# A third transpose by way of DRAM strips in the first layer's pipeline, and a new place for the router's products

## The chip, the core and the metric

The kernel runs on one core of a Trainium2 chip. The metric is the device time of one execution in microseconds (us); it is the median of repeated runs. The engines are named as in the profile: PE is TensorE's matmuls, PEld its weight loads, DVE is VectorE, ACT ScalarE, POOL GpSimd, SP SyncE, which here does nothing but issue DMA transfers. All data are float32.

## What is computed

Two layers follow each other on x of shape 4 x 1024 x 256. Each adds an attention and a feed-forward branch to x:

```python
xn = layernorm(x)
# layer 0: causal attention and a dense FFN on the same xn
q, k, v = xn @ Wq, xn @ Wk, xn @ Wv
att = softmax(where(causal, q @ k.T / sqrt(256), -inf))
x = x + layernorm(att @ v + v, gamma, beta) @ Wfc + bfc + relu(xn @ W1 + b1) @ W2 + b2

xn = layernorm(x)
# layer 1: gated attention (GAU) on layernorm(xn), and 8 experts, the best 2 per row
x = x + gau(layernorm(xn, ln1_w, ln1_b)) + experts(xn)
# experts: scores = softmax(xn @ Wg.T); of the best 2, weights scaled to sum 1
#   h1, h3 = (xn @ W1 + xn @ A1 @ B1 + b1), (xn @ W3 + xn @ A3 @ B3 + b3)
#   y = (silu(h1) * h3) @ W2 + (...) @ A2 @ B2 + b2
```

## The kernel before, in words

**Tiling.** A sequence has 1024 rows, eight tiles of 128 rows, taken in pairs. A pair tile u (0 to 15) is pair p = u % 4 of sequence b = u // 4, 256 rows. The first stage (layer 0, lines 244 to 796) is a loop over u; the second stage (from line 806) does layer 1.

**An iteration u of the first stage**, in the order of the text (lines 732 to 792) and in the order in which TensorE runs it:

- `turns` (L546): the softmax results att of u, made in the iteration before, are transposed on TensorE into PSUM (pt) and copied to attT. For p > 0 and u > 1 (`far(u)`) only the last two tiles go this way. The older part was written to DRAM (`atd`) by `bands` (L515) and read back in strips, `band`, so laid out that VectorE's transpose (which turns 32x32 blocks) leaves a full transpose. `weighted` (L556) does that transpose (L566) and multiplies attT by xn into pz: first the products with the tiles turned on TensorE (L571), then those with the band (L574).
- `hidden` (L532) in two halves: the first layer of the FFN, products pm (L539), relu on ScalarE into hT. The first half stands among the transposes at the iteration's start, the second half ahead of `finish`.
- `queries(u + 1)` (L472), then `scores(u + 1)` (L482): products sc, mask, maximum, exp, normalisation into att, of the next pair tile.
- `norms_turn(u - 1)` (L631): the result of `norms` of the pair tile before, xl, is transposed on TensorE by four instructions (L636) into PSUM and copied by ScalarE (L641), for sequence 0 into `xl0`, which stays, otherwise into `xlT`, which is also stored in DRAM (`xld`, L643) for the second stage. `logits(u - 1)` (L647) multiplies it by the router's and the qk weights (pl, L653).
- `first(u + 3)` (L439): layer norm of a later pair tile, xn. For u > 2 its xn is written to DRAM (`keep`, L429) and read back in four strips of 128-byte rows (`strip`, L436); `first_turn` (L452) turns the strips on VectorE (L455).
- `finish(u)` (L582): for each of the two tiles 8 products po with w2 (L590) and 2 products pv (L594), then the sums.
- `merge` (L393) folds an expert's low-rank factors into its weights: it loads wt and lt from DRAM early; `multiply` makes the small products pab and pc (L411 to L414), VectorE adds them to wt (L417), and two stores follow.
- `norms(u)` (L607): layer 1's two norms of the new x into xl (VectorE, L621) and xr.
- Once a sequence is through, `route` and `send` (L661, L691) pick experts and slots, and `rows_out` scatters the rows by indirect DMA on POOL's queue.

**What sets the order.** Each engine runs its instructions in the order in which they were issued. That order is not the text's own: a planner in the framework goes through all traced instructions with a model of their costs, and gives each engine next, of the instructions which it holds to be ready, the one that stands earliest in the text. `tc.issue_after(ins)` queues the instructions of its block behind `ins` on the same engine. SP is one such engine: if a DMA waits for its source, those behind it on SP wait too. A tile taken from a pool with `bufs=n` under a tag waits until one of the n slots is free.

**Slots.** att takes four slots of 4 KB per partition under the tag "att"; the bands that come back from DRAM, and `early` (rows of biases at the start), take theirs from the same four. strip has one slot, xl one, PSUM tiles named by `bank` share four banks, sc and merge's products two double banks.

Of the kernel before, what the change touches and what calls it, by code (L numbers as in the profile page):

```python
# [9 lines left out]
F32 = mybir.dt.float32  # L10
# [7 lines left out]
P = 128  # L18
B, N, D = 4, 1024, 256
NT = N // P  # L20
DC = D // P
# [4 lines left out]
E, HID, R = 8, 512, 16  # L26
# [41 lines left out]
def block_kernel(ctx: ExitStack, tc: tile.TileContext, x, wq, wk, wv, wfc, w1, w2, wqk, wvl, wg,  # L68
                 wo, wr, ew, el, eb2, cols, rows, rope, posb, out):
    nc = tc.nc  # L70
    pers = ctx.enter_context(tc.tile_pool(name="pers", bufs=1))
    small = ctx.enter_context(tc.tile_pool(name="small", bufs=3))
    NP = NT // 2
# [101 lines left out]
    yg = dram.tile([NF * TB + NHB * HB, D], F32, name="yg")  # L175
    xnd = dram.tile([B * NP, 2 * P, D], F32, name="xnd")
    atd = dram.tile([B * NP, 2 * P, (NP - 1) * 2 * P], F32, name="atd")
    xld = [dram.tile([P, DC, N], F32, name=f"xld{b}") for b in range(B)]
# [59 lines left out]
    with ExitStack() as l0:  # L238
# [7 lines left out]
        def bank(shape, name):  # L246
            return p_mm.tile(shape, F32, tag="mm", name=name)
# [17 lines left out]

        early = act.tile([P, 3 * D], F32, tag="att", name="early", bufs=4)
        nc.scalar.dma_start(out=wq_s, in_=wq)
# [125 lines left out]
        def merge(u, after):  # L393
            e, c = u // DC, u % DC
# [12 lines left out]
            def multiply():  # L407

                pab, pc = (p_sc.tile([P, 2, HID], F32, tag="sc", name=n) for n in ("pab", "pc"))
                pa, pb, pc = pab[:, 0], pab[:, 1], pc[:, 0].rearrange("p (i d) -> p i d", i=2)  # L410
                nc.tensor.matmul(pa, f1[:, ts(c, P)], f1[:, D : D + HID], start=True, stop=True)  # L411
                nc.tensor.matmul(pb, f3[:, ts(c, P)], f3[:, D : D + HID], start=True, stop=True)
                for i in range(2):
                    nc.tensor.matmul(pc[:, i, :], f2[:, ts(2 * c + i, P)], f2[:, HID : HID + D],  # L414
                                     start=True, stop=True)
                for k, p in enumerate((pa, pb, pc.rearrange("p i d -> p (i d)"))):
                    nc.vector.tensor_tensor(wt[:, k, :], p, wt[:, k, :], ALU.add)  # L417
                nc.sync.dma_start(
                    out=wm13[e, :, 0:EB1].rearrange("p (k c w) -> p k c w", k=2, c=DC)[:, :, c, :], in_=wt[:, 0:2, :])
                nc.sync.dma_start(out=wm2[e, :, ts(c, HID)], in_=wt[:, 2, :])  # L420
# [6 lines left out]

        def keep(u):
            nc.sync.dma_start(out=xnd[u].rearrange("(i p) d -> p i d", p=P), in_=xns[u])  # L429

        def strip(u):
            keep(u)
            w = strips[u] = act.tile([P, DC, 2 * P], F32, tag="strip", name="strip", bufs=1)
            src = xnd[u].rearrange("(i r) (c j a) -> j r c i a", r=32, c=DC, a=32)
            for j in range(4):
                nc.sync.dma_start(out=w[32 * j : 32 * j + 32].rearrange("r c (i a) -> r c i a", a=32), in_=src[j])  # L436


        def first(u):  # L439
# [9 lines left out]
            if u > 2:  # L449
                strip(u)  # L450

# [30 lines left out]
        def scores(u, qT):  # L482
            b, p = divmod(u, NP)
            atts = []
            for i in range(2):
# [10 lines left out]
                nc.vector.tensor_reduce(nmax, sc[:, :n], AX.X, ALU.max, negate=True)  # L496
                att = act.tile([P, N], F32, tag="att", name="att", bufs=4)
                rsum = small.tile([P, 1], F32, tag="rsum", name="rsum")
# [16 lines left out]
        def bands(u, i, att):  # L515
# [4 lines left out]
            if i == 0:  # L520
# [4 lines left out]
                bands.xn2, bands.got = xn2, []  # L525
            got = act.tile([P, N], F32, tag="att", name="band", bufs=4)[:, 0:w]
            src = there.rearrange("(i r) (j k) -> j r i k", r=32, j=4)
# [54 lines left out]
        def finish(u, hT, zT):  # L582
# [3 lines left out]
            for i in range(2):  # L586
# [6 lines left out]
                for c in range(DC):  # L593
                    nc.tensor.matmul(pv, zT[:, c, ts(i, P)], vo_s[:, c, :, :],  # L594
                                     start=(c == 0), stop=(c == DC - 1))
                nc.vector.tensor_tensor(xt, po[:, i, :], xt, ALU.add)
# [10 lines left out]
        def norms(u):  # L607
# [20 lines left out]
            nc.gpsimd.tensor_tensor(both, both, row("ln2_b").unsqueeze(1).to_broadcast([P, 2, D]), ALU.add)  # L628
            return xl

        def norms_turn(u, xl):  # L631
            b, p = divmod(u, NP)
            pt = bank([P, DC, 2 * P], "pt")
            for i in range(2):
                for c in range(DC):
                    nc.tensor.transpose(pt[:, c, ts(i, P)], xl[:, i, ts(c, P)], ident)  # L636
            if b == 0:
                xlT = xl0[:, :, ts(p, 2 * P)]
            else:
                xlT = act.tile([P, DC, 2 * P], F32, tag="xlT", name="xlT", bufs=1)  # L640
            nc.scalar.copy(xlT, pt)  # L641
            if b:
                nc.sync.dma_start(out=xld[b][:, :, ts(p, 2 * P)], in_=xlT)  # L643
            return xlT
# [87 lines left out]
        for u in range(U):  # L732
# [7 lines left out]
            if u == 1:  # L740
                for k in range(3):
                    keep(k)
                fold_second(raw)
# [15 lines left out]
            if u + 1 < U:  # L759
                qT = queries(u + 1)  # L760
            if u:
                xlT = norms_turn(u - 1, xl)
            zT = weighted(u, attT)
            if u:
                logits(u - 1, xlT, lgs)
            ready = scores(u + 1, qT) if u + 1 < U else None
            hidden(u, hT, range(IC // 4, IC // 2))
            if u + 3 < U:
                first(u + 3)
            if p == 1 and b:  # L770
                send(b - 1, *routed)
# [610 lines left out]
```

## Time and profile before

| | us |
|---|---|
| median of 3 timed runs | 1124.15 |
| lowest and highest | 1123.61, 1127.02 |
| the profiled execution, whole | 1128.42 |
| its span, first to last instruction | 1126.7 |

The granted TensorE clock was 0.998 of full speed on the mean. The first stage's last pv instruction begins at 503.0 us; layer 1's products start at 503.4 us.

TensorE's timeline gives the length of an iteration, from the start of merge's products (L411) to their next start:

| iteration | p | from, us | length, us | att read back through DRAM |
|---|---|---|---|---|
| 4 | 0 | 143.76 | 26.33 | no |
| 5 | 1 | 170.09 | 30.10 | 256 columns |
| 6 | 2 | 200.19 | 33.12 | 512 columns |
| 7 | 3 | 233.31 | 29.87 | 768 columns |

In the lines of a timeline the first number is the start in us from the span's start, the second the length of the group, then engine, line, operation and tiles (output<-inputs), the shapes, and how many of them follow each other. A bracket at the end is the idle time before it and what ended it. `SPq` is SP issuing a DMA; the transfer itself goes on afterwards. A product of float32 stands in the trace as two matmul instructions, a transpose as one; the counts are of instructions. Lines of a windows view give: the window, its length, the busy time of PE, PEld, DVE, ACT and POOL with the number of instructions, the granted clock, the mean busy share of the 16 DMA engines, and GB/s.

### The profile page before, as it was taken

Reading aid. Unit: us, or ns where it says so; the run is one execution under the profiler, and the core shown is the slowest. Engines: PE = TensorE matmul, PEld = TensorE weight load, DVE = VectorE, ACT = ScalarE, POOL = GpSimd, SP = SyncE. Lnnn points to the kernel's source line nnn. Section 1 sums busy time; section 2 is a strip of 40 time slices with the busy share of each in tenths; the row PEclk is TensorE's granted clock in tenths of the full one; section 3 lists DMA queues with packets and bytes.
Section 4 is the critical chain, followed back from the end, with each engine's and each line's share of the span. In section 5 each row is a group of like instructions: output and inputs, shape, how many; then the busy total and the mean of one; then the engine's idle time right before and its main releaser. Section 6 shows DMA issues by size and latency. Waiting matters only on the chain. (4 is left out here: it accounts for less than half of the span.)

```text
span 1126.7 us, 15401 instructions
## 1 busy us (share of the span) xinstructions
PE 1106.9 (98%) x5132; PEld 867.4 (77%) x5132; DVE 555.4 (49%) x1533; ACT 288.7 (26%) x758; POOL 177.7 (16%) x216
## 2 busy tenths in 40 slices
PE   8999999999999999999999999999999999999997
PEld 6788888888888888774688888888888884655645
DVE  5444554455444454547575623322332326677946
ACT  3323333333323333225211111111111113121121
POOL 2200002222032114141000000000000004453410
PEclk9999999999999999999999999999999999999999
DMA  8735434553455334420648786777777621322301
GB/s 308 200 100 160 129 99 149 159 178 119 132 162 155 94 128 141 158 96 33 222 101 290 212 269 190 241 227 221 238 228 223 231 85 57 121 76 75 95 28 37
DMA packets 186801, 173.77 MB, mean 154 GB/s; under 512 B 113888, under 2 KB 156384, under 8 KB 181600
## 3 DMA queue, kind: packets, MB, share of 16 engines
q1 hardware_dynamic: 99216, 137.89, 37.9%
q10 hardware_dynamic: 81360, 18.10, 7.5%
q0 software_dynamic: 6144, 16.79, 4.5%
q8 instruction: 41, 0.67, 0.3%
q14 instruction: 40, 0.33, 0.1%
HBM read 122.78 MB, written 51.02 MB: 154 GB/s over the span
## 5 line engine op out<-in xcount | busy, mean ns | idle before, releaser
L957 PE MATMUL p<-xT,w 128*128 128x256 f32 (+1 forms) x1152 | 241.2, 368 | 0.0
L957 PEld LDWEIGHTS p<-xT,w 128*128 128x128 f32 x1152 | 209.4, 190 | 26.9 <-issue 0.3
L1036 POOL DMA_INDIRECT y<-yg,slot x64 | 65.3, 1021 | 491.0 <-DVE v L1116 421.2
L962 ACT ACTIVATE s<-p,w 128x256 f32<-128x256 f32 (+1 forms) x144 | 58.8, 459 | 314.3 <-PE p L957 228.4
L965 DVE SCALAR_TENSOR_TENSOR g<-p,w,s 128x256 f32<-128x256 f32 (+1 forms) x144 | 60.8, 463 | 159.1 <-PE p L957 156.8
L978 PE MATMUL py<-w,g 128*128 128x256 f32 x544 | 123.4, 379 | 0.0
L539 PE MATMUL pm<-xnT,w_s 128*128 128x256 f32 x512 | 118.5, 379 | 0.0
L590 PE MATMUL po<-w_s,hT 128*128 128x256 f32 x512 | 116.1, 380 | 0.0
L978 PEld LDWEIGHTS py<-w,g 128*128 128x128 f32 x544 | 102.9, 190 | 14.2 <-DVE g L965 0.3
L590 PEld LDWEIGHTS po<-w_s,hT 128*128 128x128 f32 x512 | 96.9, 190 | 20.1 <-issue 8.0
L539 PEld LDWEIGHTS pm<-xnT,w_s 128*128 128x128 f32 x512 | 95.6, 192 | 11.6
L714 POOL DMA_INDIRECT xg<-xr,put x64 | 63.9, 998 | 209.0 <-ACT hT L542 138.2
L492 PE MATMUL sc<-xnT,qT 128*128 128x256 f32 (+1 forms) x320 | 65.8, 361 | 0.0
L542 ACT ACTIVATE hT<-pm,colt 128x256 f32<-128x256 f32 x128 | 53.9, 466 | 42.2 <-PE pm L539 42.2
L1114 PE MATMUL pv<-wvl_s,xl 128*128 128x512 f32 x128 | 58.1, 599 | 3.4 <-DVE v L1116 3.1
L594 PE MATMUL pv<-vo_s,zT 128*128 128x512 f32 x128 | 60.1, 592 | 0.0
L1232 PE MATMUL pj<-wo_s,gd 128*128 128x256 f32 x256 | 57.0, 381 | 2.6 <-DVE o L1234 2.1
L492 PEld LDWEIGHTS sc<-xnT,qT 128*128 128x128 f32 x320 | 54.6, 191 | 6.0 <-ACT qT L479 0.2
L1185 PE MATMUL pg<-xl,wg_s 128*128 128x512 f32 x128 | 57.5, 593 | 0.0
L1232 PEld LDWEIGHTS pj<-wo_s,gd 128*128 128x128 f32 x256 | 48.0, 190 | 10.2 <-DVE o L1234 3.3
L980 DVE TENSOR_TENSOR yt<-py,w 128x512 f32<-128x512 f32 (+1 forms) x36 | 23.8, 662 | 59.0 <-PE py L978 59.0
L603 DVE SCALAR_TENSOR_TENSOR x<-pv,rs,x 128x256 f32<-128x256 f32 x32 | 15.5, 484 | 72.1 <-ACT rs L189 47.7
(256 smaller groups left out, 1351.8 us busy)
## 6 DMA issues: line engine op xcount, KB each, us to landing
w<-wm SPq DMA_DIRECT2D x36, 1028.0 KB
w<-wm SPq DMA_DIRECT2D x36, 640.0 KB
wt<-in_ew_dram SPq DMA_DIRECT2D x16, 768.0 KB
wm<-wt SPq DMA_DIRECT2D x16, 512.0 KB
xt<-xg ACTq DMA_DIRECT2D x128, 64.0 KB
yg<-yt ACTq DMA_DIRECT2D x32, 256.0 KB
xnd<-xn SPq DMA_DIRECT2D x16, 256.0 KB
wm<-wt SPq DMA_DIRECT2D x16, 256.0 KB
```

What stands on the lines that cost most here:

```text
L492: nc.tensor.matmul(sc[:, kp * 2 * P : kp * 2 * P + w], qT[:, c, ts(i, P)], xnTs[b * NP + kp][:, c, 0:w], start=(c == 0), stop=(c == DC - 1))
L539: nc.tensor.matmul(pm[:, j, :], w1_s[:, c, ts(2 * m2 + j, P)], xnTs[u][:, c, :], start=(c == 0), stop=(c == DC - 1))
L590: nc.tensor.matmul(po[:, i, :], hT[:, m, ts(i, P)], w2_s[:, m, :], start=(m == 0), stop=(m == IC - 1))
L594: nc.tensor.matmul(pv, zT[:, c, ts(i, P)], vo_s[:, c, :, :], start=(c == 0), stop=(c == DC - 1))
L714: w = nc.gpsimd.indirect_dma_start(out=xg, out_offset=bass.IndirectOffsetOnAxis(ap=put[:, b * NT + t : b * NT + t + 1], axis=0), in_=xrs[b ...
L957: nc.tensor.matmul(p[:, j, :], w13[:, w0 : w0 + P], xT[:, c, :], start=(c == 0), stop=(c == DC - 1))
L962: nc.scalar.activation(s[:, j, :], p1[:, j, :], AF.Silu, bias=w13[:, EB1 + m : EB1 + m + 1])
L965: up.g = nc.vector.scalar_tensor_tensor(g[:, m, :], p3[:, j, :], w13[:, EB3 + m : EB3 + m + 1], s[:, j, :], ALU.add, ALU.mult).ins
L978: down.last = nc.tensor.matmul(py[:, k, :], g[:, m, ts(k, P)], w2[:, m * D : (m + 1) * D], start=(m == 0), stop=(m == EC - 1)).ins
L1036: w = nc.gpsimd.indirect_dma_start(out=ys[b][:, t, k, :], out_offset=None, in_=yg, in_offset=bass.IndirectOffsetOnAxis(ap=slot[:, n : n + ...
L1114: nc.tensor.matmul(pv, a.xl[:, c, ts(t, P)], wvl_s[:, c, :], start=(c == 0), stop=(c == DC - 1))
L1232: nc.tensor.matmul(pj, a.gd[:, m, ts(n, P)], wo_s[:, m, :], start=(m == 0), stop=(m == HC - 1))
```

## The change

It touches the first stage alone.

- xl of sequences 0 to 2 (pair tiles 0 to 11) is written to a new DRAM tensor `xlr` at the end of `norms`, read back in strips as xn is, and turned on VectorE straight into xl0 or xlT. The four TensorE transposes, their PSUM bank and ScalarE's copy stay for sequence 3 alone. `keep` and `strip` now take the place and the rows as arguments; `strip` returns its tile.
- For these pair tiles `norms_turn` and `logits` stand behind the second half of `hidden` and `first(u + 3)` in the text, ahead of `send` and of `finish` with its po products, instead of around `weighted`. In iterations 13 to 15 they stay where they were.
- `merge`'s products are queued behind the last pv product of `finish` (`finish.last`), in all iterations but the last.
- att gets two slots of its own, the bands that come back two smaller ones (768 columns, tag "band", shared with `early`), strip two slots instead of one.

```diff
--- before.py
+++ after.py
@@ -174,6 +174,7 @@
     xg = dram.tile([E * RS, D], F32, name="xg")
     yg = dram.tile([NF * TB + NHB * HB, D], F32, name="yg")
     xnd = dram.tile([B * NP, 2 * P, D], F32, name="xnd")
+    xlr = dram.tile([B * NP, 2 * P, D], F32, name="xlr")
     atd = dram.tile([B * NP, 2 * P, (NP - 1) * 2 * P], F32, name="atd")
     xld = [dram.tile([P, DC, N], F32, name=f"xld{b}") for b in range(B)]
 
@@ -263,7 +264,7 @@
             for _ in range(n):
                 keep_busy.last = nc.tensor.matmul(pw, idle[:, 0:P], idle, start=True, stop=True).ins
 
-        early = act.tile([P, 3 * D], F32, tag="att", name="early", bufs=4)
+        early = act.tile([P, 3 * D], F32, tag="band", name="early", bufs=2)
         nc.scalar.dma_start(out=wq_s, in_=wq)
         load_x(0, 0)
         nc.sync.dma_start(out=wk_s, in_=wk)
@@ -408,11 +409,12 @@
 
                 pab, pc = (p_sc.tile([P, 2, HID], F32, tag="sc", name=n) for n in ("pab", "pc"))
                 pa, pb, pc = pab[:, 0], pab[:, 1], pc[:, 0].rearrange("p (i d) -> p i d", i=2)
-                nc.tensor.matmul(pa, f1[:, ts(c, P)], f1[:, D : D + HID], start=True, stop=True)
-                nc.tensor.matmul(pb, f3[:, ts(c, P)], f3[:, D : D + HID], start=True, stop=True)
-                for i in range(2):
-                    nc.tensor.matmul(pc[:, i, :], f2[:, ts(2 * c + i, P)], f2[:, HID : HID + D],
-                                     start=True, stop=True)
+                with tc.issue_after(finish.last) if u + 1 < U else nullcontext():
+                    nc.tensor.matmul(pa, f1[:, ts(c, P)], f1[:, D : D + HID], start=True, stop=True)
+                    nc.tensor.matmul(pb, f3[:, ts(c, P)], f3[:, D : D + HID], start=True, stop=True)
+                    for i in range(2):
+                        nc.tensor.matmul(pc[:, i, :], f2[:, ts(2 * c + i, P)], f2[:, HID : HID + D],
+                                         start=True, stop=True)
                 for k, p in enumerate((pa, pb, pc.rearrange("p i d -> p (i d)"))):
                     nc.vector.tensor_tensor(wt[:, k, :], p, wt[:, k, :], ALU.add)
                 nc.sync.dma_start(
@@ -425,15 +427,16 @@
 
 
 
-        def keep(u):
-            nc.sync.dma_start(out=xnd[u].rearrange("(i p) d -> p i d", p=P), in_=xns[u])
-
-        def strip(u):
-            keep(u)
-            w = strips[u] = act.tile([P, DC, 2 * P], F32, tag="strip", name="strip", bufs=1)
-            src = xnd[u].rearrange("(i r) (c j a) -> j r c i a", r=32, c=DC, a=32)
+        def keep(there, rows):
+            nc.sync.dma_start(out=there.rearrange("(i p) d -> p i d", p=P), in_=rows)
+
+        def strip(there, rows):
+            keep(there, rows)
+            w = act.tile([P, DC, 2 * P], F32, tag="strip", name="strip", bufs=2)
+            src = there.rearrange("(i r) (c j a) -> j r c i a", r=32, c=DC, a=32)
             for j in range(4):
                 nc.sync.dma_start(out=w[32 * j : 32 * j + 32].rearrange("r c (i a) -> r c i a", a=32), in_=src[j])
+            return w
 
 
         def first(u):
@@ -447,7 +450,7 @@
             for i in range(2):
                 normalise(xn[:, i, :], xb[:, 2 * p + i, :], mv, rstd, i)
             if u > 2:
-                strip(u)
+                strips[u] = strip(xnd[u], xn)
 
         def first_turn(u):
             if u in strips:
@@ -494,7 +497,7 @@
                 nc.vector.tensor_tensor(sc[:, ts(t, P)], sc[:, ts(t, P)], causal, ALU.add)
                 nmax = small.tile([P, 1], F32, tag="nmax", name="nmax")
                 nc.vector.tensor_reduce(nmax, sc[:, :n], AX.X, ALU.max, negate=True)
-                att = act.tile([P, N], F32, tag="att", name="att", bufs=4)
+                att = act.tile([P, N], F32, tag="att", name="att", bufs=2)
                 rsum = small.tile([P, 1], F32, tag="rsum", name="rsum")
                 nc.scalar.activation(att[:, :n], sc[:, :n], AF.Exp, bias=nmax, accum_out=rsum)
                 rinv = small.tile([P, 1], F32, tag="rinv", name="rinv")
@@ -523,7 +526,7 @@
                 for j in range(4):
                     nc.sync.dma_start(out=xn2[32 * j : 32 * j + 32, 0 : 2 * p, :], in_=src[j])
                 bands.xn2, bands.got = xn2, []
-            got = act.tile([P, N], F32, tag="att", name="band", bufs=4)[:, 0:w]
+            got = act.tile([P, (NP - 1) * 2 * P], F32, tag="band", name="band", bufs=2)[:, 0:w]
             src = there.rearrange("(i r) (j k) -> j r i k", r=32, j=4)
             for j in range(4):
                 nc.sync.dma_start(out=got[32 * j : 32 * j + 32].rearrange("r (i k) -> r i k", i=4), in_=src[j])
@@ -591,8 +594,8 @@
                                      start=(m == 0), stop=(m == IC - 1))
                 pv = bank([P, 2, D], "pv")
                 for c in range(DC):
-                    nc.tensor.matmul(pv, zT[:, c, ts(i, P)], vo_s[:, c, :, :],
-                                     start=(c == 0), stop=(c == DC - 1))
+                    finish.last = nc.tensor.matmul(pv, zT[:, c, ts(i, P)], vo_s[:, c, :, :],
+                                                   start=(c == 0), stop=(c == DC - 1)).ins
                 nc.vector.tensor_tensor(xt, po[:, i, :], xt, ALU.add)
                 sq = act.tile([P, D], F32, tag="sq", name="sq", bufs=1)
                 var = small.tile([P, 1], F32, tag="var", name="var")
@@ -626,19 +629,23 @@
 
             both = xs[b][:, 2 * p : 2 * p + 2, :]
             nc.gpsimd.tensor_tensor(both, both, row("ln2_b").unsqueeze(1).to_broadcast([P, 2, D]), ALU.add)
-            return xl
+
+            return strip(xlr[u], xl) if b < B - 1 else xl
 
         def norms_turn(u, xl):
             b, p = divmod(u, NP)
-            pt = bank([P, DC, 2 * P], "pt")
-            for i in range(2):
-                for c in range(DC):
-                    nc.tensor.transpose(pt[:, c, ts(i, P)], xl[:, i, ts(c, P)], ident)
             if b == 0:
                 xlT = xl0[:, :, ts(p, 2 * P)]
             else:
                 xlT = act.tile([P, DC, 2 * P], F32, tag="xlT", name="xlT", bufs=1)
-            nc.scalar.copy(xlT, pt)
+            if b < B - 1:
+                nc.vector.transpose(xlT, xl)
+            else:
+                pt = bank([P, DC, 2 * P], "pt")
+                for i in range(2):
+                    for c in range(DC):
+                        nc.tensor.transpose(pt[:, c, ts(i, P)], xl[:, i, ts(c, P)], ident)
+                nc.scalar.copy(xlT, pt)
             if b:
                 nc.sync.dma_start(out=xld[b][:, :, ts(p, 2 * P)], in_=xlT)
             return xlT
@@ -739,7 +746,7 @@
                 raw = second(qTs[0])
             if u == 1:
                 for k in range(3):
-                    keep(k)
+                    keep(xnd[k], xns[k])
                 fold_second(raw)
             hT = act.tile([P, IC, 2 * P], F32, tag="hT", name="hT", bufs=1)
             if u == 0:
@@ -758,15 +765,18 @@
             multiply = merge(u, qTs[u])
             if u + 1 < U:
                 qT = queries(u + 1)
-            if u:
+            late = u <= U - NP
+            if not late:
                 xlT = norms_turn(u - 1, xl)
             zT = weighted(u, attT)
-            if u:
+            if not late:
                 logits(u - 1, xlT, lgs)
             ready = scores(u + 1, qT) if u + 1 < U else None
             hidden(u, hT, range(IC // 4, IC // 2))
             if u + 3 < U:
                 first(u + 3)
+            if u and late:
+                logits(u - 1, norms_turn(u - 1, xl), lgs)
             if p == 1 and b:
                 send(b - 1, *routed)
```

## The prediction

> **What bounds the kernel now.** I read the page's first two parts, then TensorE's own waits and timeline in the first stage, then VectorE, SyncE (SP) and DMA at the places which the change touches. The page says that TensorE is busy nearly throughout, and a window over iterations 1 to 14 of the first stage (52 to 473 us) shows it without a gap; the list of TensorE's waits in that window is empty.
>
> ```profile
> span 1126.7 us, 15401 instructions
> PE 1106.9 (98%) x5132; PEld 867.4 (77%) x5132; DVE 555.4 (49%) x1533; ACT 288.7 (26%) x758; POOL 177.7 (16%) x216
> ```
> ```profile
> 52.00:473.00 421.00, 421.00 (x2034) 345.25 (x2032) 203.21 (x645) 139.02 (x425) 81.39 (x74) 1.00 0.46 139
> ```
>
> So in this stage a product taken off TensorE is worth its full time, unless what follows it then waits. In the second stage TensorE is bound too, and what it does there follows the first stage's end, so a gain arrives whole. Iteration 4, one with p = 0, from the timeline (start, length, engine, line):
>
> ```profile
> 149.08 0.73 DVE L621 TENSOR_SCALAR xl<-x,mean,rstd 128x256 f32<-128x256 f32 x2
> 150.40 0.60 PE L636 MATMUL pt<-ident,xl 128*128 128x128 f32 x4
> 150.84 1.47 PE L571 MATMUL pz<-attT,xn 128*128 128x256 f32 x8
> 151.66 0.60 SPq L403 DMA_DIRECT2D wt<-in_ew_dram  x1
> 152.17 1.11 PE L653 MATMUL pl<-wqr_s,xl 128*128 128x72 f32 x8
> 153.12 3.25 PE L492 MATMUL sc<-xnT,qT 128*128 128x256 f32 x16
> 158.02 0.36 SPq L519 DMA_DIRECT2D atd<-att  x1
> ```
>
> **What goes.** Four transposes of xl take 150.84 - 150.40 = 0.44 us from start to start (the 0.60 is a pipelined end). They go for pair tiles 0 to 11, that is in iterations 1 to 12: 12 x 0.44 = 5.3 us. Each copy of their result (L641, 0.60 us on ScalarE) goes too, worth nothing: ScalarE is a quarter busy.
>
> The Trainium skill ("Perfetto Trace Analysis", Engine Utilization) calls matmul busy time a bad metric because matmuls are pipelined; by the busy time the four would count 4 x 0.273 = 1.1 us and the sum 13 us. The starts in the trace decide for 0.44.
>
> **What comes.** The product pl moves from behind pz to ahead of po. It takes 152.17 to 153.12 = 0.95 us here and 127.67 to 128.52 = 0.85 in iteration 3, wherever it stands: at most 0.1 x 3 gained. A VectorE transpose of 128x512 (L455, 0.70 us each) comes, 12 x 0.70 = 8.4 us on an engine that is busy 203 of these 421 us: nothing, as long as its input has landed. Behind it in VectorE's queue stand the softmax of the next pair tile, which TensorE reads only in the next iteration, and zT, needed only behind the first 16 po instructions; that cover is about 3 us.
>
> SP gets five more issues: one write of 0.38 us, four reads of 0.63, 2.9 us in iterations of 26 to 33, and a hold of about 1.8 us while the write lands. Behind that hold stand the wt load (used some 20 us later) and the write of xn (used an iteration later): nothing.
>
> **Does xl arrive in time?** The same way is walked by xn today, in the iteration before:
>
> ```profile
> 130.25 0.38 SPq L429 DMA_DIRECT2D xnd<-xn  x1
> 132.40 2.59 SPq L436 DMA_DIRECT2D strip<-xnd  x4
> ```
> ```profile
> 133.70:136.60 2.90, 2.90 (x16) 2.54 (x15) 0.29 (x1) 1.05 (x4) 0.00 (x0) 1.00 0.57 90
> 152.80:157.10 4.30, 4.30 (x26) 3.89 (x26) 3.91 (x15) 0.52 (x2) 1.27 (x1) 1.00 0.78 244
> ```
>
> The write takes 2.15 us until the first read goes out; the reads' 262 KB flow at 90 GB/s until 136.6, 1.6 us behind the last issue at 134.99. In iteration 4 xl is ready at 149.08 + 0.73 = 149.81. Alone: write at 149.87, landed 152.02; the wt load stands before the reads until 152.26; reads 152.3 to 154.9, landed 156.5, transposed 157.3. pl's new place is po's start 159.66 less 0.44 less 0.95 = 158.3: in time by 1 us. But wt's 786 KB fill the DMA engines first: at the second window's 244 GB/s from 152.9 to 156.1. The strips then end between 156.1 + 262 KB / 244 = 157.2 and 156.1 + 2.9 = 159.0, and xlT stands between 158.0 and 159.8. So TensorE waits between 0 and 1.5 us in each of the three p = 0 iterations (4, 8, 12); I take 0.3, 0.9 in all, near the faster end, since by the trace's packet times 361 of wt's 384 packets have begun by 155.8. With p = 1, 2, 3 pl's place is 17.9 to 21.3 us behind the end of the last pv (po's start there less 0.44, pl and, with p = 1, prk), xl is ready 6 us behind it, and the way takes 8 to 10: no wait.
>
> The skill speaks against it: "DMA: Bandwidth & Descriptors", Specifications, wants 512 B for line rate, and these reads move 128 B. As an estimate from that page, if each packet cost as much as one of 512 B, the reads would take four times the faster end's 1.1 us: xlT at 161.2, 2.9 us of wait per p = 0 iteration, 8.7 in all, and a sum of +3.4. The first window above, 90 GB/s over 2.9 us, is what small packets cost here, and it decides.
>
> **What is late next.** With p = 3 the next thing is the turned band. Iteration 3:
>
> ```profile
> 118.87 0.42 DVE L554 COPY attT<-pt 128x256 f32<-128x256 f32 x1
> 119.21 0.73 DVE L621 TENSOR_SCALAR xl<-x,mean,rstd 128x256 f32<-128x256 f32 x2
> 119.85 1.83 DVE L566 STREAM_TRANSPOSE attT<-band 128x768 f32<-128x768 f32 x2
> 120.53 0.60 PE L636 MATMUL pt<-ident,xl 128*128 128x128 f32 x4
> 120.97 0.82 PE L571 MATMUL pz<-attT,xn 128*128 128x256 f32 x4
> 121.73 2.86 PE L574 MATMUL pz<-attT,xn 128*128 128x256 f32 x12
> ```
>
> The band is turned at 121.68 and L574 starts at 121.73, already 0.1 us behind the end of L571's four (120.97 + 0.66). Without the transposes L571 ends at 121.19 and TensorE would wait 0.54: iterations 3, 7 and 11 would gain nothing, 1.3 us lost of the 5.3, unless the planner puts other products there. With p = 2 the band is turned 7.19 us behind the last pv, and L574 could start at 7.22; with p = 1 there is 0.5 us to spare. Does the planner fill? In iteration 15, where the same products came too early, it did:
>
> ```profile
> 479.40 0.82 PE L571 MATMUL pz<-attT,xn 128*128 128x256 f32 x4
> 480.15 1.12 PE L411 MATMUL pab<-lt 16*128 16x512 f32 x2
> 481.20 2.86 PE L574 MATMUL pz<-attT,xn 128*128 128x256 f32 x12
> ```
>
> Merge's products may no longer fill (they are held behind the last pv), but the second half of hidden (L539, 0.22 us each) is ready. I take the gap as filled, 0 lost, bounds 0 and 1.3.
>
> **Edits that cost nothing.** Merge behind the last pv: it stands there already in iterations 0 to 14 (pab at 113.89, behind pv). Two slots for att: att is read by turns at 115 to 117 and the next is written at 130. Two for the band: turned by 121.7, reloaded behind 130. Two strips: one each for xn and xl in flight. The xld store goes some 6 us later; the second stage reads it. route starts some 6 us later in p = 0 iterations (153.6 now); what it feeds on TensorE, prk, stands at 189.31, 30 us on. If that cover went, route's small VectorE pieces would fall ahead of the band's transposes, at most 0.5 us three times. DMA gains 6.3 MB where its share is 0.46.
>
> **Sum.** -5.3 + 0.9 = -4.4 us on the span of 1126.7, so 1122.3, and 1124.0 for the profiled run's 1128.42 with the 1.7 us around the span. That run lies above the median of the timed runs, 1124.15; the difference carries over: **1119.8 us**. All at the best end (5.3, 0.3 of pl, 0.3 of the gap already there) gives -5.9, 1118.2.
>
> **Rivals.**
> 1. *The gain is eaten at both waits.* No fill in p = 3 (1.3) and pl 0.5 to 1.5 us late in p = 0 (1.5 to 4.5): -2.5 to +0.5, about 1122.8. For it: the reads' way past wt ends within 1.5 us of the place. Against it: the planner fills elsewhere. Chance 0.25, no change that can be told.
> 2. *SP's order (slower).* xl's reads are put behind the first write of att, as xn's were in iteration 6, where the write stood at 211.27 and the reads far back:
>
> ```profile
> 211.27 0.39 SPq L429 DMA_DIRECT2D xnd<-xn  x1
> 219.72 0.34 SPq L519 DMA_DIRECT2D atd<-att  x1
> 226.04 1.29 SPq L436 DMA_DIRECT2D strip<-xnd  x2
> ```
>
>    In iteration 4 the reads would go out at 158.4, land at 162.6 and be turned at 163.4, 5.1 us late; three times 15.3 less 5.3 gives +10, 1134. It decides from (5.3 + 3.4) / 3 = 2.9 us late per p = 0 iteration. Against it: xl's reads stand earlier in the program text than the write of att, xn's stand later. Chance 0.15.
> 3. *The change doesn't do what it says*: the planner holds xlT for later than it is and puts pl behind po. Then no wait, 1118.8; it belongs to the faster side.
>
> **Chances and range.** What a measurement can tell from no change is 0.3%, 3.4 us: 1120.8 to 1127.5. Forecast with rival 3: faster 0.60; rival 1: same 0.25; rival 2: slower 0.15. The forecast's own range is 1117.5 to 1120.8 (the best end with 0.7 for the runs' spread); to leave out no more than 2 in 10 it reaches over rival 1, to 1126.
>
> **What would show it.** Right: L636's transposes on TensorE 16 times, not 64; pl ahead of po in iterations 1 to 12 with idle time of at most 1.5 us, at p = 0 alone; products of L539 between L571 and L574 at p = 3; first-stage end near 499 us, not 503.4. Wrong: pl waiting for the transpose with p = 1 or 2; VectorE held at the strip long enough that zT delays pv; L574 waiting for the band.

## The result, and the profile after

The changed kernel takes **1137.09 us** (median of 4 runs, 1134.92 to 1138.83) against 1124.17 (4 runs): a ratio of **1.0104, 95% interval 1.0092 to 1.0117**. It is slower by 12.9 us; forecast was faster by 4.4. The page after, its first and busiest lines, and TensorE's waits and the sum of a window over iterations 1 to 14:

```profile
span 1133.8 us, 15373 instructions
PE 1107.5 (98%) x5084; PEld 864.1 (76%) x5084; DVE 562.1 (50%) x1545; ACT 282.5 (25%) x746; POOL 176.3 (16%) x216
```
```profile
52.00:483.00 431.00, 422.42 (x1987) 341.69 (x1989) 209.99 (x654) 132.78 (x414) 80.52 (x74) 0.99 0.52 150
```
```profile
engine line waited for: us in total, times, longest us
PE pl L660 <- DVE xlT L642: 5.0, 6, 1.6
PE pl L660 <- DVE xl L642: 2.5, 2, 2.3
PE po L593 <- DVE x L599: 0.6, 1, 0.6
...
PE pz L577 <- DVE attT L569: 0.2, 1, 0.2
```

The 48 transposes are gone (5132 to 5084 instructions). The window, which had no gap before, has 8.6 us of them now, nearly all pl's (its line is L660 now) waiting for VectorE's new transpose of the strips (L642).

The length of each iteration (end of the last pv to the next such end), in us:

```
p   iterations   before                  after less before        sum
1   1, 5, 9      34.05, 30.10, 30.10     +0.02, +0.59, +0.60      +1.2
2   2, 6, 10     33.11, 33.11, 33.11     -0.31, -0.32, -0.32      -0.9
3   3, 7, 11     29.87, 29.88, 29.88     +4.02, +2.74, +3.23     +10.0
0   4, 8, 12     26.33, 26.32, 26.32     -0.08, -0.08, -0.07      -0.2
    0; 13 to 15                          -0.2; 0.0                -0.2
    first stage ends at 503.6 before, 513.4 after                 +9.8
```

So **the loss lies in the three p = 3 iterations**, and the other nine, due to gain 0.44 each, gain nothing together. The two profiles differ by 7.1 us in span, the medians by 12.9. Their second stages, the same code, took 623.1 us before and 620.4 after, a difference such as there is between chips: in the runs below, before's median is 1125.2 and 1125.6 us on two chips and 1128.2 on two others, and the second stage takes 619.7 to 620.8 us in the profiles from the first two and 622.9 to 623.6 in those from the others. So 9.8 us, the first stage's, is what the two profiles put down to the change. The first stage's lengths don't go with the chip: run 1 repeats those of before to 0.02 us. The changed kernel's own runs spread with the granted clock: spans 1133.2, 1133.8, 1137.0, 1137.1 at 0.996, 0.995, 0.992, 0.991.

**Iteration 3 after**, TensorE (columns as in the timelines before; line numbers are those of each run's own kernel; a time with a plus sign, like +6.0, is in us behind the end of the last pv of the iteration before):

```profile
120.02 0.82 PE L574 MATMUL pz<-attT,xn 128*128 128x256 f32 x4
120.67 0.60 PE L542 MATMUL pm<-xnT,w_s 128*128 128x256 f32 x2
121.29 1.58 PE L495 MATMUL sc<-xnT,qT 128*128 128x128 f32 x8
122.70 1.03 PE L542 MATMUL pm<-xnT,w_s 128*128 128x256 f32 x4
123.60 2.86 PE L577 MATMUL pz<-attT,xn 128*128 128x256 f32 x12
126.29 0.82 PE L574 MATMUL pz<-attT,xn 128*128 128x256 f32 x4
126.95 2.76 PE L577 MATMUL pz<-attT,xn 128*128 128x256 f32 x12
129.54 2.32 PE L542 MATMUL pm<-xnT,w_s 128*128 128x256 f32 x10
134.20 1.31 PE L660 MATMUL pl<-wqr_s,xl 128*128 128x72 f32 x8 [2.34 <-DVE xl L642]
135.30 5.16 PE L593 MATMUL po<-w_s,hT 128*128 128x256 f32 x16
```

The planner did fill between L574 and the band's L577, but with 3 us of work, not 0.5: 6 of hidden's 16 instructions and all of sc. Behind pz only 10 of hidden are left as cover, that is as work which TensorE does while pl's input is on its way, and pl waits 2.34 us. VectorE in the same iteration:

```profile
119.34 0.97 DVE L569 STREAM_TRANSPOSE attT<-band 128x768 f32<-128x768 f32 x1
122.04 0.30 DVE L497 TENSOR_TENSOR sc<-sc,causal 128x128 f32<-128x128 f32 x1 [1.73 <-PE sc L495]
...
122.58 0.97 DVE L569 STREAM_TRANSPOSE attT<-band 128x768 f32<-128x768 f32 x1
...
129.74 0.69 DVE L580 TENSOR_TENSOR zT<-pz,xnT 128x512 f32<-128x512 f32 x1 [1.23 <-PE pz L577]
130.35 0.74 DVE L183 BATCH_NORM_STATS2 st<-x 128x6 f32<-128x256 f32 x2
...
133.36 0.69 DVE L642 STREAM_TRANSPOSE xl<-strip 128x512 f32<-128x512 f32 x1
```

Before, both bands were turned back to back from 119.85. Now the second stands behind the mask of the next scores (L497), for which VectorE idles 1.73 us. xl's strips had landed at 128.2, but L642 stands behind zT (which needs all of pz) and behind eight tiles' statistics of sequence 2 (L183), that `first` takes in one go in this iteration. Then the granted clock falls to one half for 3.41 us; it is the number after the last bracketed count in each of these lines (1.00, 0.50, 1.00):

```profile
131.80:134.20 2.40, 0.06 (x2) 0.03 (x1) 2.25 (x10) 2.00 (x8) 0.00 (x0) 1.00 0.85 199
134.91:138.32 3.41, 3.41 (x11) 2.85 (x11) 0.99 (x3) 0.00 (x0) 0.00 (x0) 0.50 0.69 226
138.32:141.00 2.68, 2.68 (x12) 2.09 (x11) 0.42 (x1) 0.00 (x0) 0.00 (x0) 1.00 0.00 0
```

po's first 16 take 5.16 us where 3.62 is usual. In iteration 11 it is the same: a wait of 1.49, then a clock of 0.50 from 380.67 to 384.08 and 5.35 for po.

**Iteration 7** shows SP. Before, the second band's four reads went out in iteration 6 (228.05), ahead of merge's first store (236.71). After:

```profile
240.42 0.39 SPq L420 DMA_DIRECT2D wm<-wt  x1
240.91 3.49 SPq L532 DMA_DIRECT2D band<-atd  x4
244.44 2.59 SPq L438 DMA_DIRECT2D strip<-xnd  x4
247.13 0.56 SPq L422 DMA_DIRECT2D wm<-wt  x1
247.79 0.38 SPq L431 DMA_DIRECT2D xlr<-xl  x1
```

The last pv of iteration 6 ended at 237.08. SP stood still from 229.0 until merge's sums (VectorE, L419) were there, with the band's reads behind the store; xl, ready at +6.0, is written only at +10.7.

```profile
248.14 0.35 DVE L505 TENSOR_SCALAR att<-att,rinv 128x256 f32<-128x256 f32 x1
248.66 0.98 DVE L569 STREAM_TRANSPOSE attT<-band 128x768 f32<-128x768 f32 x1 [0.17 <-issue]
```

The last landing of the second band's reads that the trace has is at 246.55 (+9.5); VectorE turns the band at +11.6, behind the softmax of the next scores (L505). L577 starts at +12.6, not +7.8, with all 16 of hidden used up ahead of it; pl waits 1.61. In iteration 11 the reads again follow the store, landing at +8.3, and the band is turned at +11.3. In iteration 3 the last landing on the trace is at 114.2, so there the order on VectorE alone makes the second band late.

### The profile page after: what moved, and what is told of

It reads as the page before. It is cut to its first block, busy times and chain, and to the rows that moved or that the text cites. A ratio compares the mean times of both kernels' runs of the same rounds, so it can differ in the third digit from the quotient of the medians.

```text
span 1133.8 us, 15373 instructions
## 1 busy us (share of the span) xinstructions
PE 1107.5 (98%) x5084; PEld 864.1 (76%) x5084; DVE 562.1 (50%) x1545; ACT 282.5 (25%) x746; POOL 176.3 (16%) x216
## 5 line engine op out<-in xcount | busy, mean ns | idle before, releaser
L593 PE MATMUL po<-w_s,hT 128*128 128x256 f32 x512 | 119.9, 388 | 0.6 <-DVE x L599 0.6
L721 POOL DMA_INDIRECT xg<-xr,put x64 | 63.0, 984 | 217.2 <-ACT hT L545 151.2
L606 DVE SCALAR_TENSOR_TENSOR x<-pv,rs,x 128x256 f32<-128x256 f32 x32 | 15.5, 484 | 70.0 <-ACT rs L190 51.1
```

The lines of the kernel that those rows point to most:

```text
L593: nc.tensor.matmul(po[:, i, :], hT[:, m, ts(i, P)], w2_s[:, m, :], start=(m == 0), stop=(m == IC - 1))
L721: w = nc.gpsimd.indirect_dma_start(out=xg, out_offset=bass.IndirectOffsetOnAxis(ap=put[:, b * NT + t : b * NT + t + 1], axis=0), in_=xrs[b ...
```

## Experiments

Fourteen kernels ran. The diffs below are excerpts, and `...` marks what is left out. "To before" is the ratio to the kernel before on the same chip, with its interval; the last four columns are the sums over iterations of one p (each three of them), after less before, in us, from the profiles (-1.3 would be 3 x 0.44).

```
run                              us       to before                 p=1    p=2    p=3    p=0
the change                     1137.09  1.0104 [1.0092, 1.0117]    +1.2   -0.9  +10.0   -0.2
1 slots and merge alone        1128.19  1.000  [0.999,  1.001]      0.0    0.0    0.0    0.0
2 strips not for p=3           1130.30  1.0018 [1.0008, 1.0027]    +1.2   -0.9   +1.0   +0.6
3 no strips, xl turned late    1141.59  1.0145 [1.0128, 1.0162]    +3.7   +3.9   +5.0   +3.6
4 zero products ahead of pl    1131.43  1.0055 [1.0039, 1.0072]    +1.2   -0.9   +5.7   -0.2
5 statistics behind xl's       1132.66  1.0061 [1.0045, 1.0078]    +1.2   -0.9   +6.5   -0.2
6 pl between the two tiles     1134.32  1.0076 [1.0059, 1.0093]    -1.0   -0.9  +12.6   -0.8
7 as 5, stores behind bands    1140.67  1.0120 [1.0103, 1.0137]    +1.2   -0.9  +12.1   -0.2
8 as 7, pl between             1140.31  1.0110 [1.0090, 1.0130]    +0.4   -0.5  +11.5   +1.3
9 xl's way on POOL             1157.19  1.0265 [1.0246, 1.0283]    -1.3   -1.2  +10.6  +17.4
10 as 9, pl between            1133.63  1.0049 [1.0037, 1.0062]    -1.3   +0.1   +4.1   +0.8
11 as 10, statistics behind    1131.11  1.0025 [1.0016, 1.0035]    -1.3   +0.5   +1.7   +1.3
12 xl's way on ScalarE         1132.21  1.0060 [1.0045, 1.0076]    -1.3   -1.2   +0.3   +7.3
13 as 12, pl between           1121.64  0.9970 [0.9960, 0.9980]    -1.3   -1.2   -0.1   -1.5
14 strips at p=0, 1, pl between 1122.24 0.9973 [0.9962, 0.9985]    -1.3    0.0    0.0   -1.5
```

**Which part costs (1, 2, 3).** Run 1 keeps the change's slots and merge's place alone:

```diff
-            return strip(xlr[u], xl) if b < B - 1 else xl
+            return xl
...
-            late = u <= U - NP
+            late = not u
```


> The slots (two for att, two smaller ones for the bands, two for strip) and the queueing of merge's products behind the last pv stay; xl is turned on TensorE for all pair tiles at the place it had in the kernel before, and nothing of it goes through DRAM. If these parts of the change cost nothing, as the prediction had it: the time of before, 1124 to 1126, all iterations within 0.3 us of before. If the narrower slots or the merge's place are what costs in iterations 3, 7 and 11: 1130 or more, with 2 to 3 us lost in each of the three.

1.000, every iteration within 0.02 us of before. Those edits are free; the strips and the late place make the loss. Run 2:

```diff
+        def by_strips(u):
+            return u // NP < B - 1 and u % NP != 2
...
-            late = u <= U - NP
+            late = not u or by_strips(u - 1)
...
```


> xl of pair tiles 2, 6 and 10, which are turned in iterations 3, 7 and 11, goes over TensorE at its old place; the other nine keep the strips and the late place. Theory: the whole loss lies in the three p = 3 iterations, and the other nine gain 0.1 to 0.3 each, so 1.5 in all: 1120 to 1124. Rival, the loss is spread or is a general one (DMA load, clock, the second stage): 1130 or more.

Most of the loss is gone, 1.0018 against 1.0104, though the other nine don't gain the 1.5 us that was put; they lose 0.9 together. Even without strips of xl in the p = 3 iterations L577 starts at +10.9, +13.0 and +13.0 there: the strips of the iteration before stand on SP ahead of the bands, and in iteration 7 the second band's reads (238.51) again follow merge's store (238.02). It costs only 0.33 each, since pl at its old place needs no cover. Run 3:

```diff
-            return strip(xlr[u], xl) if b < B - 1 else xl
+            return xl
...
-            if b < B - 1:
-                nc.vector.transpose(xlT, xl)
-            else:
-                pt = bank([P, DC, 2 * P], "pt")
...
+            pt = bank([P, DC, 2 * P], "pt")
...
```


> The changed kernel with xl turned on TensorE for all pair tiles, as before; the new place of pl, merge's queueing and the slots stay. Theory A: pl has its input early, no wait, 1123 to 1126. Theory C (slots, merge's place or the planner's new order by themselves cost the time): above 1130.

This one does not isolate the place as meant: the transposes moved too, and pl, straight behind them, waits for the copy of their result in each of twelve iterations.

```profile
162.43 0.60 PE L644 MATMUL pt<-ident,xl 128*128 128x128 f32 x4
163.99 1.11 PE L657 MATMUL pl<-wqr_s,xl 128*128 128x72 f32 x8 [0.97 <-ACT xl L645]
```

It does show that at the late place nothing stands between pl and what it waits for.

**The clock (4).** Eight products with zeros ahead of pl in iterations 3, 7 and 11:

```diff
+                if p == NP - 1:
+                    with tc.issue_after(hidden.last):
+                        pw = bank([P, D], "pw")
+                        for _ in range(4):
+                            filler = nc.tensor.matmul(pw, zero[:, 0:P], zero, start=True, stop=True).ins
...
```


> The changed kernel with four products of zeros (8 instructions, 1.7 us) ahead of pl in iterations 3, 7 and 11, so that TensorE is not idle while it waits there; results unchanged. If the idle time itself brings the clock down (0.70 over 5 us behind pl in iterations 3 and 11): pl starts no later, the clock stays at 1.0 behind it, about 3 us less than the changed kernel in the profile and 3 to 6 in the timed runs, 1131 to 1134. If the clock has nothing to do with it: the same 1135 to 1139.

```profile
131.17 1.89 PE L784 MATMUL pw<-zero 128*128 128x256 f32 x8
133.67 1.08 PE L660 MATMUL pl<-wqr_s,xl 128*128 128x72 f32 x8 [0.61 <-DVE xl L642]
134.59 3.67 PE L593 MATMUL po<-w_s,hT 128*128 128x256 f32 x16
```

pl waits 0.61 us behind them and po takes 3.67, not 5.16. The three iterations lose 5.7 us instead of 10.0, and with eight products that compute nothing in each of them the ratio goes from 1.0104 to 1.0055, which is 5.5 us; the granted clock of its runs is 0.998 to 0.999, not 0.991 to 0.996. Of the 1.7 us that iterations 3 and 11 each win back, po's speed is 1.5 and 1.7.

**Who is late (5 to 8).** Run 5 moves the eight statistics behind xl's transpose on VectorE:

```diff
-            for i in range(2):
-                first.stats = stats(xb[:, 2 * p + i, :], mv, i, "st0")
+            with tc.issue_after(norms_turn.of[u // NP]) if u >= 2 * NP else nullcontext():
+                for i in range(2):
+                    first.stats = stats(xb[:, 2 * p + i, :], mv, i, "st0")
...
```


> The changed kernel with one order changed on VectorE: the eight layer-norm statistics of the sequence after next, which stand ahead of xl's transpose in iteration 3, are queued behind it (in iteration 7 behind it too). If VectorE's order is what makes pl wait 2.3 us in iteration 3, its strip being in SBUF 5 us before: iteration 3 shrinks from 33.9 to about 30 us (2.3 of wait and 1.5 of lower clock), the whole by 3 to 4 us to 1132 to 1135, iterations 7 and 11 stay near 32.6 and 33. If the transfer is late there: no change, 1135 to 1139.

```profile
129.55 0.69 DVE L581 TENSOR_TENSOR zT<-pz,xnT 128x512 f32<-128x512 f32 x1 [1.23 <-PE pz L578]
130.15 0.70 DVE L643 STREAM_TRANSPOSE xl<-strip 128x512 f32<-128x512 f32 x1
130.78 0.71 DVE L183 BATCH_NORM_STATS2 st<-x 128x6 f32<-128x256 f32 x2
```

Iteration 3 goes from +4.02 to -0.22: there the statistics were the last of the chain. Iterations 7 and 11 stay at +3.50 and +3.24. Run 6:

```diff
+                if between and i == 0:
+                    with tc.issue_after(finish.last):
+                        between()
...
-                logits(u - 1, norms_turn(u - 1, xl), lgs)
+                xlT = norms_turn(u - 1, xl)
+                between = lambda: logits(u - 1, xlT, lgs)
...
```


> The strips stay; only the router's products pl move from ahead of the first tile's po to behind the first tile's pv, some 5 us later on TensorE. Theory A (pl's place: TensorE stands at pl until VectorE has turned xl's strip, 7.6 us in all in the changed kernel, and at p = 3 the granted clock falls after it): the waits go, TensorE keeps the 5 us of transposes, 1117 to 1121 us. Theory B (the strips' own load on DMA, SP and VectorE slows the stage): stays above 1130.

With po and pv of a tile as cover, all nine iterations with p = 0, 1, 2 gain 0.07 to 0.48. At p = 3 the sum is worse (iteration 3 loses less, 1.2 us, but 7 and 11 lose 4.9 and 6.5): with pl due later xl's transpose stands at +27 to +31, and pl waits 1.1 to 3.0 there. Run 7, on run 5:

```diff
+                with tc.issue_after(bands.last) if far(u + 1) and u + 1 < U else nullcontext():
+                    nc.sync.dma_start(
+                        out=wm13[e, :, 0:EB1].rearrange("p (k c w) -> p k c w", k=2, c=DC)[:, :, c, :], in_=wt[:, 0:2, :])
+                    nc.sync.dma_start(out=wm2[e, :, ts(c, HID)], in_=wt[:, 2, :])
...
```


> As the run with the statistics behind xl's transpose, and besides merge's two stores are queued on SP behind the last read of the bands, so that SP no longer waits for merge's sums with the second band's reads behind it. Theory (SP's order is what costs in iterations 7 and 11): the reads go out in iterations 6 and 10, the second band is turned within 8 us of the last pv, the write of xl goes out at +6, and iterations 7 and 11 lose under 0.7 us each against before instead of 3.2 to 3.5: 1124 to 1127. Rival (the cost there is something else, VectorE's order or the planner's use of hidden): both stay above +2.5, 1131 to 1133.

The theory as put there fell. Iteration 7 lost 1.81 instead of 3.50: the band's reads go out in iteration 6 and xl's write at +6.0, as expected, yet the second band is still turned at +11.6 and L577 starts at +12.6, as VectorE still has it behind the softmax of the next scores. So the order on VectorE, and not the reads' date alone, holds it there; that the planner reckoned with a late band would explain the order, but its dates aren't on record. Iteration 11 lost 10.5:

```profile
360.34 0.46 SPq L432 DMA_DIRECT2D xnd<-xn  x1
372.40 0.32 SPq L529 DMA_DIRECT2D xn<-xnd  x1
372.88 0.62 SPq L404 DMA_DIRECT2D wt<-in_ew_dram  x1
373.59 2.60 SPq L439 DMA_DIRECT2D strip<-xlr  x4
```

A read into xn2 (L529) waits 11.5 us on SP for pz to leave that tile, with xl's reads behind it; pl waits 7.8. Run 8 adds pl's place between the tiles to run 7:

> As the run before it, and pl besides between the two tiles of finish (behind tile 0's pv). If what is left then is the wait for xl's transpose that stands late in VectorE's order (0.18 in p = 0, 0.79 in p = 1), each of the twelve iterations gains 0.3 to 0.45 against before and the time is 1118 to 1121, below the kernel before. If the planner answers with other waits (po, pv): 1123 or more.

It misses 1118 to 1121 by far, and other waits come, as the second case had it: pl waits 1.1, 1.1 and 3.0 in the p = 3 iterations and 1.1 in iteration 9, sc 1.8 in iteration 8, and pz, pv and po 1.4, 0.8 and 0.6 in iteration 11.

**Another queue (9 to 14).** Run 9 leaves the changed kernel as it is and lets POOL issue xl's write and reads (`keep` and `strip` take the queue as an argument):

```diff
-            return strip(xlr[u], xl) if b < B - 1 else xl
+            return strip(xlr[u], xl, nc.gpsimd) if b < B - 1 else xl
...
```


> The changed kernel with one difference: xl's write to DRAM and its four strip reads are issued by POOL's queue, not SP's. Theory (the five issues on SP, and what they do to SP's order and to the planner's date for the second band, make the loss): TensorE's order in iterations 3, 7 and 11 is that of before again, the band's products at +7.4 to +7.8 behind the last pv, and the three iterations stand within 0.7 us of before; the first stage ends at 503 to 505 and the time is that of before within 0.15%. If VectorE's own order (the statistics ahead of xl's transpose, the transpose late) is enough to keep the loss: iterations 3, 7, 11 still lose 2 or more each and the ratio stays above 1.006. If POOL's queue is too slow or is held (by its own sums or the scatter): pl waits in other iterations too.

The order came back, the time did not. L577 starts at +7.6 in all three p = 3 iterations, iteration 11 gains 0.16, and p = 1 gains the full 0.44 three times. But the way on POOL's queue is slow; in iteration 8:

```profile
280.80 1.27 POOL L631 TENSOR_TENSOR x<-x,rowt 128x512 f32<-128x512 f32 x1
282.01 0.77 POOL L431 DMA_DIRECT2D xlr<-xl  x1
283.08 1.00 POOL L721 DMA_INDIRECT xg<-xr,put  x1 [0.30 <-issue]
288.70 2.76 POOL L438 DMA_DIRECT2D strip<-xlr  x4 [4.62 <-DMA xlr<-xl]
```

The write goes out behind POOL's own sum (at +8.0, not +6.0), shares its queue with the scatter (L721), and takes 6.7 us until the first read; SP's took 2.1. pl waits 5.8 there. Runs 10 and 11 put pl between the tiles on top of that, the second with the statistics behind, too:

> As the run with xl's way on POOL's queue, and pl between the two tiles of finish besides. If the theory holds, nothing waits any more, each of the iterations 1 to 12 gains 0.30 to 0.48 against before as nine of them did with pl in this place, and the ratio to before is 0.996 (4 to 5 us). If not, 1.0 or more, with the waits named in the trace.

> As the run before it, with the later sequence's statistics also queued behind xl's transpose of iterations 3 and 7. If those statistics still hold xl's transpose there, this one is 0.5 to 2 us below the run before it; if pl between the tiles covers them, the two are equal.

1.0049 and 1.0025: better than run 9, but 0.996 is missed. po now waits for hT (4.6 us in run 10). Run 11 is 2.5 us below run 10, a little more than the 0.5 to 2 put. Run 12 is run 9 with ScalarE's queue (`nc.scalar`):

> The changed kernel with one difference: xl's write and its four strip reads are issued by ScalarE's queue, not SP's. With POOL's queue TensorE's order in iterations 3, 7 and 11 was that of before, but POOL itself was held by its sums and the scatter. If the five issues on SP are the whole cause of the loss in the p = 3 iterations: each of the three stands within 0.7 us of before, pl's waits are those behind VectorE's order alone (0.2 at p = 0, 0.8 at p = 1), and the time is 1.000 +- 0.0015 of before. If ScalarE's queue is held as POOL's was (by the write's landing, some 2 us, with relu and exp behind it): waits of po for hT or of turns for att, 1.005 or more. If VectorE's order keeps the loss by itself, iterations 3 and 7 still lose 2 or more in pl's wait.

The p = 3 iterations are at +0.33, 0.00 and 0.00: **taking the five issues off SP removes the loss there**. No edit touches VectorE's order, yet that order changed too: in iteration 3 both bands are turned by +7.6 again, and five of the eight statistics stand ahead of xl's transpose, not eight:

```profile
120.43 2.86 PE L577 MATMUL pz<-attT,xn 128*128 128x256 f32 x12 [0.25 <-DVE attT L569]
130.67 0.70 DVE L642 STREAM_TRANSPOSE xl<-strip 128x512 f32<-128x512 f32 x1
131.52 1.08 PE L660 MATMUL pl<-wqr_s,xl 128*128 128x72 f32 x8 [0.23 <-DVE xl L642]
```

Its ratio of 1.0060 is a miss, and "held as POOL's was" is nearer to it, though the wait is pl's: ScalarE's reads land later, xl is turned at +15.5 to +16.1 with p = 0 instead of +13.9, and pl straight ahead of po waits 1.8 to 2.4 in iterations 4, 8 and 12; in 8 the clock fell besides. Run 13 gives pl its cover:

> As the run with ScalarE's queue, and pl between the two tiles of finish. If the transposes' 0.44 us per iteration is there to be had once SP's order and the direct wait of pl are both out of the way: iterations 1 to 12 each gain 0.30 to 0.48 and the ratio to before is 0.996 +- 0.0015, below both kernels. If ScalarE's work behind the held queue is the next wait: 1.000 or more.

```profile
157.15 3.62 PE L593 MATMUL po<-w_s,hT 128*128 128x256 f32 x16
160.60 1.88 PE L597 MATMUL pv<-vo_s,zT 128*128 128x512 f32 x4
162.32 1.01 PE L663 MATMUL pl<-wqr_s,xl 128*128 128x72 f32 x8
```
```profile
engine line waited for: us in total, times, longest us
PE pz L577 <- DVE attT L569: 1.0, 3, 0.4
PE pt L650 <- DVE xl L627: 1.0, 2, 0.8
```

**1121.64 us, 0.997 [0.996, 0.998]**: below both kernels. No wait of pl is left. Nine iterations gain 0.31 to 0.49. Those with p = 3 gain 0.14, 0.01 and 0.00: what the transposes leave there is 0.25 to 0.40 us of waiting for the band. The first stage ends at 499.2, 4.4 us earlier. Run 14 stays on SP's queue and takes strips only where no band is delayed:

```diff
+            return u // NP < B - 1 and u % NP in (0, NP - 1)
...
```


> Strips on SP's queue for the six pair tiles alone that are turned in iterations with p = 0 and 1 (4, 5, 8, 9, 12 and 1); xl of the others is turned on TensorE at its old place; pl of the six between the two tiles of finish. No strip of xl stands on SP in iterations with p = 2 or 3, so the second band keeps its date. Theory: the p = 2 and 3 iterations are those of before within 0.1 us, the six gain 0.26 to 0.45 each, 2.1 in all: ratio 0.998. If strips in any iteration delay the bands: above 1.0.

The p = 2 and 3 iterations are those of before to 0.01 us, the other six gain 0.44 to 0.49: 1122.24, 0.9973 [0.9962, 0.9985]. Runs 13 and 14 can't be told apart.

## Why the prediction was wrong

**Right:** the transposes' price. Where nothing waits, most iterations gain 0.44 to 0.49 (runs 9 to 14); with both causes of waiting away, twelve iterations gain 4.1 us by the table (run 13). Run 13 moves the same bytes through DRAM as the change, so the added DMA traffic by itself isn't the loss. Slots, bands, att and merge cost nothing, as put (run 1). p = 0 waited 0.18 three times by the brackets, within the 0 to 1.5 given; by the starts of the groups the wait cost 0.35, so that only 0.08 was gained there. (The Trainium skill's words on matmul busy time, which the prediction cites from "Perfetto Trace Analysis", stand in that page's opening note and under "Identifying the Most-Contended Engine", not under "Engine Utilization".)

**Wrong: "SP gets five more issues ... nothing".** This is the step that failed. The issues' own 2.9 us and the hold behind the write were counted; what they are queued ahead of was not followed past the wt load and xn's write. With them on SP, the second band of the p = 3 iterations is turned 2.3 to 4.8 us later: in all three it stands behind next scores' work on VectorE, and in 7 and 11 its reads come late too, behind merge's store. Run 7 shows that early reads alone don't bring it forward in iteration 7. Off SP, or without strips in the iterations with p = 2 and 3, all of that is gone (runs 12 and 14). How the five issues lead the planner to this order stays open.

**Wrong: "I take the gap as filled, 0 lost".** It was filled, but what fills is hidden's second half, the very work that stood between pz and pl as cover. 6, 16 and 16 of its 16 instructions went that way, and pl at its new place then waited 2.3, 1.6 and 1.5 us. Filling a gap and covering a wait were counted as if the same 3.6 us could do both. In run 13, where pl has other cover, the planner leaves the gap unfilled, and it eats 1.2 us of the 1.3 that these three iterations were to gain, nearly the other bound given.

**Wrong: "With p = 1, 2, 3 ... no wait".** When the strips land was reckoned rightly (+12 to +15 but for 7 and 11); but a landing isn't a transpose. L642 stands where the planner puts it on VectorE: behind zT and the statistics with p = 3, at +17.9 with p = 1, where pl waits 0.79. That the other place for pl brings p = 1 its 0.44 shows that this wait was the price there (run 14 in all three iterations, run 6 in 1 and 5).

**Missing: the clock.** No term for it stood in the sum. In the profile it is 3.2 us, what po lost in iterations 3 and 11 (1.5 and 1.7). In the timed runs it is at most the 5.5 us between the ratios of the change and of run 4, which hold shorter waits too (0.9 us in iteration 7 of the profiles, where the clock doesn't fall).

Rival 2 had the side right and the mechanism nearly: SP's order, but the bands' reads behind a store in p = 3, not xl's reads behind att's write in p = 0. Another order for the band on VectorE alone, with all strips left on SP, was not tried.

## What to carry to other kernels

A transfer added to an in-order issue queue costs what comes due behind it, in the next iteration, too: follow each read that it pushes back to its user, above all those near a store that waits for a late source. Cover is spent once; before moving a product to a place, count what stands between it and its input after the planner has filled the other gaps. If an engine's queue is the trouble, try the same transfers from another engine's queue before giving the idea up.

## What was unexpected of the hardware

The granted clock fell to 0.50 for 3.41 us, from 134.91 and from 380.67, behind TensorE waits of 2.34 and 1.49 us (iterations 3 and 11), yet not behind one of 1.61 (iteration 7, po 3.67). At half speed 3.41 us do 1.7 us less work, and po took 1.5 and 1.7 us longer. In the 3.41 us ahead of the two falls TensorE was busy for 1.07 and 1.92 us. The two falls begin 245.76 us apart, 72 times 3.413; counted off in the same steps, the wait of iteration 7 lies in 254.38 to 257.79, where TensorE was busy for 1.80 us and no fall followed. So the length of a wait doesn't decide, nor does the busy time so counted; what does stays open. In run 12 the clock fell behind 0.79 in iteration 15 (0.50 from 486.03 to 489.45; L577's twelve took 4.54 us, not 2.86), a wait that the kernel before has as well without a fall in its profile. The Trainium skill ("TensorE: Matmul & The Clock Gate", Part 1) has the clock halved after an idle window of about 3.4 us; the half and the 3.41 us agree with these falls, but they came behind waits of 0.79 to 2.34 us.

With what stood between them on the queue, xl's reads went out 2.1 to 3.2 us behind the write from SP's queue (the change), 2.1 to 3.9 from ScalarE's (run 13) and 3.0 to 7.1 from POOL's (run 9).
